# Scores of layer 0's paired panels on VectorE, the first panel's list one unit later, and lone panels normalized by VectorE, in a two-layer graph network with experts

## The chip, the cores and the metric

The kernel is one program on one core of a Trainium2 chip. The metric is the device time of one execution, in microseconds (us). The kernel before was timed three times: 1230.33, 1235.99 and 1239.86 us, median 1235.99 us. One further execution was taken by the hardware profiler; it took 1232.09 us and is the source of every duration below.

## The reference

There are N = 3327 nodes with D = 256 features, a dense matrix `adj` of 3327 x 3327 with few non-zeros, and two layers. Each layer is a graph step, followed by a step of 8 experts of which every node uses two.

```python
def _L0_gnn_ref(x, adj, W, b):
    return relu(matmul(adj, matmul(x, W)) + b)
def _L0_ffn_ref(x, Wg, bg, W1, b1, W2, b2):
    gate_scores = einsum('bsd,ed->bse', x, Wg) + bg      # 8 scores for each node
    topk_scores, topk_idx = top_k(gate_scores, 2)
    topk_probs = softmax(topk_scores, axis=-1)
    ...
    for e in range(8):
        h = relu(x @ W1[e].T + b1[e])                    # 256 -> 1024
        out = out + combine[..., e:e + 1] * (h @ W2[e].T + b2[e])
...
x = x + _L0_gnn_ref(_layernorm(x), adj, L0_gnn_W, L0_gnn_b)
x = x + _L0_ffn_ref(_layernorm(x), ...)
x = x + _L1_gnn_ref(_layernorm(x), adj, adj, ...)        # adjacency tanh(adj * adj), 700 largest of a row
x = x + _L1_ffn_ref(_layernorm(x), ...)                  # 8 experts, gelu, two of them for each node
```

The change touches layer 0's graph step and what is computed beside it for layer 0's experts: the normalization of the new `x`, the gate's scores, and the lists of nodes for each expert.

## The kernel before, in words

**Tiles, panels and units.** The nodes are padded to 3328, which is 26 tiles of 128. The graph step produces the output in 13 panels of 256 nodes (two tiles each). For one panel the kernel needs a strip of 3328 x 256 of `adj`, which it loads in two pieces of 13 x 256 columns per partition (1.66 MB each). Six such pieces fit in on-chip memory and form a ring; a piece's place is loaded again as soon as its last reader is done. Layer 0's panels are grouped into units: panels 0 and 1 alone, then the pairs (2,3), (4,5), (6,7), (8,9), (10,11), then panel 12 alone.

**The product of a lone panel** (`rest`, L495) is direct: 26 tiles times two halves of the features. **The product of a pair** (`pair`) uses a scheme of seven products in place of eight: sums and differences of the pieces of `adj` are made on VectorE (`add_pieces`, L480), those of the features once (`sum_features`), and the seven products (`product`, L470) are added up in four PSUM banks. Their results go to `g1` and `g2`, partly by copies on ScalarE (`copy`, L538), partly by corrections on VectorE (L587, L603, L604). A matmul in fp32 appears as two records of about 0.2157 us each.

**What follows a unit is done in the next one.** In the first product of a unit, after its matmuls 1, 4, 7 and 10, `weigh` multiplies the sums of the unit before by the layer's weights (L506, into two PSUM buffers) and `add_relu` (L403, L404, VectorE) adds the result to `x`. For a lone panel the same is done by `finish`, a few tiles after the unit's start. Then the following steps work on the tiles of the unit before:

- *Normalization* (`route0`, `normalized`): statistics on VectorE (L337 to L349), then `scaled` (L360), one operation per tile on ScalarE.
- *Scores.* For a pair, the first two tiles are scored on VectorE: one operation per tile and expert multiplies the normalized tile with the gate's row and sums it (L659; each is followed by a short read of the accumulator). The other two tiles are turned by TensorE (`turned_tiles`, L387, two transposes per tile), copied from PSUM by ScalarE (L388), multiplied with the gate's weights on TensorE (L669) and copied by VectorE (L678). For a lone panel both tiles are scored on VectorE.
- *Ranks and weights* (`weights`, L717 on): the two best scores of each node, and a softmax of the two, whose exponential is on ScalarE (L725).
- *List* (`list_tokens`), one unit later: GpSimd writes the weights, the node numbers and a second copy of the row beside the normalized rows (three copies, from L754 on), TensorE counts the places (L760, L761), VectorE makes indices of them (L762 to L768), and GpSimd issues four indirect DMAs for two tiles, which scatter the rows to the experts' lists in HBM (L779). After the list of panels 8 and 9 an early plan (`plan_early`) is made on VectorE and GpSimd, which assigns the first blocks of nodes to experts.

**Other work in the same stretch.** `count` (L1371, ScalarE) counts the positive entries of each raw piece before `add_pieces` overwrites it. `fill` writes zeros into the spare rows of a list: a memset, an iota and a copy on GpSimd, and 16 DMAs on SP's queue (L1334, L1336), which also loads the pieces of `adj`. `begin` calls it at panel 1 for layer 0's list and at panel 4 for layer 1's. Panel 12's unit is followed by the first step of layer 0's experts. Its 16 products of the first weight matrix (`ps_h`, L1171) go to two PSUM buffers and are evicted by ScalarE with the activation (L1178); the last panel's `finish` is called between this step's two halves.

**What sets the order.** The kernel is written in Python, and a scheduler orders the instructions of each engine according to their dependences and the order of the source. The source steers it by generators: `route0` is a generator with three `yield`s, and each `next(routing)` in `pair` puts the next part of it at that place among the products. Each engine then runs its instructions in order, so that an instruction that waits holds all behind it. Buffers are reused in rings: three for the normalized tiles `xn` (two tiles each), two of `ph` (for `ps_o`, `ps_h`), four of `py` (the sums), two of `pt` (transposes, scores, places).

Of the kernel before, what the change touches and what calls it, by code (L numbers as in the profile page):

```python
# [10 lines left out]
F32 = mybir.dt.float32  # L11
# [11 lines left out]
P = 128  # L23
# [3 lines left out]
DC = D // P  # L27
E = 8
# [99 lines left out]
def gnn_moe_two_layers(  # L128
# [353 lines left out]
    def aggregate_first(b_sb, w, w_sb, begin, count, route, listed, freed):  # L482
# [85 lines left out]
        def pair(p1, p2, ps_x, ps_q, ps_b, ps_z):  # L568
            a11, a12, a21, a22 = (piece(pan, k) for pan in (p1, p2) for k in range(NCHUNK))
            b11, b21, b22 = half(0, 0), half(1, 0), half(1, 1)  # L570
            t3, t2, t4, t1 = half_sums
            hooks, pans = finishing()
            product(ps_x, b11, a11, hooks=hooks)
            g1, g2 = sums_of(), sums_of()
            copy(g1[:, 0, :], ps_x)
            add_pieces(a11, a21)
            add_pieces(a21, a22)
            count_next()
            listed()
# [12 lines left out]
            free(p2, 0)  # L592
            product(ps_x, t2, a22, first=False)
            copy(g1[:, 1, :], ps_x)
            free(p2, 1)
            count_next()
            product(ps_z, b22, a12, first=False)
            free(p1, 1)
            count_next()
            product(ps_x, t3, a11, first=False, hooks={3: lambda: next(routing)})  # L600
            for _ in routing:
                pass
            nc.vector.tensor_tensor(g1[:, 1, :], g1[:, 1, :], ps_z, ALU.add)  # L603
            nc.vector.scalar_tensor_tensor(  # L604
                g2, g2, -1.0, ps_x.unsqueeze(1).to_broadcast([P, DC, PW]), ALU.mult, ALU.subtract
            )
            free(p1, 0)
            waiting.extend([(p1, g1), (p2, g2)])

# [134 lines left out]
    routed = []  # L744
# [607 lines left out]
    g1_wg_sb = const.tile([P, DC, D], F32, name="g1_wg_sb")  # L1352
    f1_r_sb = const.tile([P, DC, E], F32, name="f1_r_sb")
    f1_b1_sb = const.tile(list(f1_b1.shape), F32, name="f1_b1_sb")
    f0_wg_sb = const.tile([P, DC, E], F32, name="f0_wg_sb")
    g1_bp_sb = const.tile(list(g1_bp.shape), F32, name="g1_bp_sb")
    for t, w in [
        (gnn_b_sb, g0_b[0:1, :].partition_broadcast(P)),
        (g1_wg_sb, g1_wg.rearrange("(c p) n -> p c n", p=P)),
        (f1_r_sb, f1_rT.rearrange("(c p) n -> p c n", p=P)),  # L1360
        (f1_b1_sb, f1_b1),
        (g1_bp_sb, g1_bp),
        (f0_wg_sb, f0_wgT.rearrange("(c p) n -> p c n", p=P)),
    ]:
        follow(nc.gpsimd.dma_start(out=t, in_=w), last_normalized)

# [17 lines left out]
    def route0(pans):  # L1384
        if pans[0] == 0:
            load_gate(gates[0])
        t, n = tiles_of(pans)
        xns = normalized(t, n, on_scalar=True)
        yield
        by_product = 2 if n == 4 else 0  # L1390
        sc = scores(xns, n - by_product, n)
        yield
        if by_product:
            scores_by_product(by_features(xns[1], 2, "h2T"), 2, f0_wg_sb, sc[:, 2:4, :])
        yield
        routed.append((xns, *weights(sc, n, f0_bg_sb), t, n, xlist0, "0"))

    def listed0():
        if not routed:
            return  # L1400
        last = routed[-1][4] + routed[-1][5]
        list_waiting()
# [447 lines left out]
```

## Time and profile before

| what | value |
| --- | --- |
| three runs, us | 1230.33, 1235.99, 1239.86 |
| profiled execution, us | 1232.09 |
| its span, first to last instruction, us | 1230.4 |
| mean granted TensorE clock | 0.985 |
| TensorE busy, 0 to 104.1 us (panels 0 to 3) | 97.87 of 104.10 |
| TensorE busy, 104.1 to 289.1 us (pairs (4,5) to (10,11)) | 180.75 of 185.00, clock 0.98 |
| VectorE busy, 104.1 to 289.1 us | 135.70 |
| ScalarE busy, 104.1 to 289.1 us | 104.77 |
| TensorE busy, 289.1 to 360 us (panel 12, first expert steps) | 65.27 of 70.90, clock 0.98 |
| TensorE busy, 360 to 561 us (experts of layer 0) | 200.94 of 201.00, clock 1.00 |
| score operations L659 on VectorE, 104 to 360 us | 96, mean 443 ns; 96 reads of the accumulator, mean 81 ns |

How to read a profile of this kind: PE is TensorE, DVE is VectorE, ACT is ScalarE, POOL is GpSimd and SP the engine that issues most of the DMAs. A group of instructions is written with its line in the kernel, its operation, the tile that it writes and the tiles that it reads, the count (x), and busy time and mean. "Idle before" is the time for which the engine stood idle just before instructions of this group, and the arrow names the engine and line that ended the idle time. The granted clock is the share of TensorE's full rate that the throttle gave; where it is below 1.00, matmuls take longer, and TensorE still counts as busy. A table of stretches gives the length of each, and the busy time of each engine in it with the number of instructions.

### The profile page before, as it was taken

To read this page: it belongs to the slowest core of one execution; us is meant where nothing else is said; L and a number is where in the kernel's file an instruction comes from. 1 tells how busy PE (TensorE), PEld (TensorE's weight loads), DVE (VectorE), ACT (ScalarE), POOL (GpSimd) and SP (SyncE) were. 2 spreads that over 40 slices of the span, in tenths; PEclk is the share of its full clock that TensorE was granted. 3 is DMA by queue.
4 is the path that set the end of the run, shared out by engine and by line. 5 is a ranking of instruction groups with operands and counts; after the bars stand their busy time and mean duration, and the time that the engine had idled before them with its cause. 6 is when DMAs were issued, how large, how long until landed. Compare 5 with 4: busy or idle time off the path is not lost. (4 is left out here: it accounts for less than half of the span.)

```text
span 1230.4 us, 18162 instructions
## 1 busy us (share of the span) xinstructions
PE 1181.0 (96%) x5749; PEld 1010.8 (82%) x5749; DVE 719.5 (58%) x2609; ACT 531.0 (43%) x988; POOL 286.9 (23%) x368
## 2 busy tenths in 40 slices
PE   8999999999999999999999999999999999989973
PEld 7878888888878888888888888888888888868862
DVE  6797687596572111211111358389999998775454
ACT  5689556540222222222232235994554552033321
POOL 1212131242231111110111110004223233255531
PEclk9999999999999999999999999999999999999997
DMA  9899634534366556657575736235544551467796
GB/s 340 189 299 281 221 127 148 202 119 163 108 202 236 181 200 202 219 184 254 180 247 190 282 157 269 101 127 190 184 163 168 184 185 63 143 207 219 224 291 204
DMA packets 123209, 241.60 MB, mean 196 GB/s; under 512 B 24496, under 2 KB 93152, under 8 KB 116192
## 3 DMA queue, kind: packets, MB, share of 16 engines
q1 hardware_dynamic: 108656, 205.59, 51.1%
q0 software_dynamic: 11168, 31.61, 6.8%
q10 hardware_dynamic: 3280, 3.15, 0.7%
q8 instruction: 48, 0.79, 0.3%
q14 instruction: 57, 0.47, 0.1%
HBM read 203.99 MB, written 36.33 MB: 195 GB/s over the span
## 5 line engine op out<-in xcount | busy, mean ns | idle before, releaser
L440 PE MATMUL ps_g<-s,ring 128*128 128x256 f32 x1352 | 294.2, 380 | 0.0
L440 PEld LDWEIGHTS ps_g<-s,ring 128*128 128x128 f32 x1352 | 256.0, 190 | 34.4
L1178 ACT ACTIVATE pad<-ps_h,ring 128x256 f32<-128x256 f32 (+1 forms) x282 | 128.5, 457 | 331.0 <-PE ps_h L1171 309.0
L1171 PE MATMUL ps_h<-pad,ring 128*128 128x256 f32 (+1 forms) x1184 | 255.1, 368 | 8.8 <-ACT pad L1161 5.4
L1171 PEld LDWEIGHTS ps_h<-pad,ring 128*128 128x128 f32 x1184 | 203.3, 191 | 53.4 <-ACT pad L1178 14.6
L1209 PE MATMUL ps_y<-ring,pad 128*128 128x256 f32 x928 | 209.4, 381 | 0.0
L779 POOL DMA_INDIRECT ys<-pad,index x114 | 112.1, 983 | 387.4 <-DVE pad L1217 246.8
L1209 PEld LDWEIGHTS ps_y<-ring,pad 128*128 128x128 f32 x928 | 173.5, 191 | 22.2 <-ACT pad L1178 0.2
L659 DVE SCALAR_TENSOR_TENSOR rt_product<-xn,gate 128x256 f32<-128x256 f32 x320 | 160.6, 502 | 14.2 <-ACT xn L360 3.6
L779 POOL DMA_INDIRECT xlist<-xn,rt_idx x104 | 112.7, 1084 | 173.4 <-DVE ln_nw L347 52.0
L1371 ACT ACTIVATE sign<-ring,below 128x416 bf16<-128x416 f32 x208 | 133.4, 642 | 11.7 <-DMA ring<-in_adjT 5.8
L470 PE MATMUL ps_g<-ring,pad 128*128 128x256 f32 x520 | 121.0, 390 | 0.2 <-DMA ring<-in_adjT 0.2
L470 PEld LDWEIGHTS ps_g<-ring,pad 128*128 128x128 f32 x520 | 100.2, 195 | 14.4 <-DMA ring<-in_adjT 0.6
L1216 DVE TENSOR_TENSOR pad<-ps_y,ring 128x256 f32<-128x256 f32 x64 | 27.1, 423 | 137.3 <-PE ps_y L1209 133.5
L1540 ACT ACTIVATE ring<-ring 128x3328 f32<-128x3328 f32 x22 | 65.4, 2979 | 87.3 <-DVE ring L1539 56.3
L1161 DVE COPY pad<-ptb 128x512 f32<-128x512 f32 (+1 forms) x29 | 18.9, 653 | 143.5 <-PE ptb L1157 143.5
L470 PE MATMUL ps_g<-ring,s 128*128 128x256 f32 x390 | 90.6, 382 | 0.0
L470 PEld LDWEIGHTS ps_g<-ring,s 128*128 128x128 f32 x390 | 75.0, 192 | 10.5
L480 DVE TENSOR_TENSOR ring<-ring,ring 128x768 f32<-128x768 f32 (+1 forms) x80 | 79.8, 1014 | 0.4 <-ACT sign L1371 0.4
L495 PE MATMUL ps_g<-ring,s 128*128 128x256 f32 x312 | 70.4, 386 | 2.6 <-ACT s L360 2.6
L495 PEld LDWEIGHTS ps_g<-ring,s 128*128 128x128 f32 x312 | 59.9, 194 | 11.5 <-ACT s L360 3.2
L1541 ACT ACTIVATE ring<-ring 128x3328 f32<-128x3328 f32 x22 | 65.4, 2978 | 0.6
(224 smaller groups left out, 1119.5 us busy)
## 6 DMA issues: line engine op xcount, KB each, us to landing
ring<-in_adjT SPq DMA_DIRECT2D x50, 1664.0 KB
ring<-in_f_w1T SPq DMA_DIRECT2D x30, 1024.0 KB
ring<-in_f_w2T SPq DMA_DIRECT2D x30, 1024.0 KB
ring<-xlist SPq DMA_DIRECT2D x52, 258.0 KB
ring<-in_f_w SPq DMA_DIRECT2D x36, 256.0 KB
ring<-ys SPq DMA_DIRECT2D x12, 512.0 KB
ring<-in_f_b SPq DMA_DIRECT2D x34, 128.0 KB
xlist<-h2T SPq DMA_DIRECT2D x16, 257.0 KB
```

The lines of the kernel that those rows point to most:

```text
L440: nc.tensor.matmul(ps[it], lhsT=chunks[k][:, c, ts(it, P)], rhs=s[:, j, :], start=(j == 0), stop=(j == NT - 1),)
L470: nc.tensor.matmul(ps, lhsT=b[:, c, :], rhs=a[:, c, :], start=(first and c == 0), stop=(c == CJ - 1), skip_group_check=not first,)
L480: nc.vector.tensor_tensor(out[:, part, :], out[:, part, :], other[:, part, :], ALU.add)
L495: nc.tensor.matmul(sums[pan][c], lhsT=s[:, j, ts(c, P)], rhs=piece(pan, j // CJ)[:, j % CJ, :], start=(j == 0), stop=(j == NT - 1),)
L659: nc.vector.scalar_tensor_tensor(product, xn, 1.0, gate[:, e, :], ALU.mult, ALU.mult, accum_out=sc[:, g, e : e + 1],)
L779: d = nc.gpsimd.indirect_dma_start(out=a[:, :], out_offset=bass.IndirectOffsetOnAxis(ap=index, axis=0), in_=rows_, in_offset=None,)
L1171: nc.tensor.matmul(ps, lhsT=w1[:, c, ts(hc, P)], rhs=xT[:, c, :], start=(c == 0), stop=(c == DC - 1),)
L1178: nc.scalar.activation(hT[:, hc, :], ps, func, bias=bb1[:, hc : hc + 1])
L1209: last_product[:] = [nc.tensor.matmul(ps, lhsT=hT[:, hc, ts(g, P)], rhs=w2[:, hc, :], start=(hc == 0), stop=(hc == hc_n - 1),)]
L1371: nc.scalar.activation(sign, piece(pan, k)[:, :, ts(i, GROUP)], AF.Sign, bias=below, accum_out=positive[:, pan, i, k : k + 1],)
L1540: nc.scalar.activation(a, a, AF.Square)
L1541: nc.scalar.activation(a, a, AF.Tanh)
```

## The change

The change has six edits, all in layer 0's part.

1. All four tiles of a pair are scored on VectorE (L659): 32 operations per pair in place of 16. The transposes (L387), ScalarE's copy (L388), the product (L669) and VectorE's copy (L678) of a pair's last two tiles are left out, with the weights `f0_wg_sb` and their load.
2. In `pair`, the corrections of `g1` and `g2` are written ahead of the rest of `route0` (ranks and weights); the addition to `g1` comes straight after the sixth product, and the hook in the seventh product goes.
3. `route0` has two `yield`s in place of three, so that all scores are in one part.
4. The list of panel 0 is not made in the unit after its scores, but together with panel 1's, in the unit of pair (4,5).
5. Lone panels are normalized by VectorE (`layernorm`, L371 in the new file), pairs by ScalarE as before.
6. Layer 1's list is filled at panel 8 instead of panel 4.

```diff
@@ def pair
             product(ps_z, b22, a12, first=False)
             free(p1, 1)
             count_next()
-            product(ps_x, t3, a11, first=False, hooks={3: lambda: next(routing)})
+            nc.vector.tensor_tensor(g1[:, 1, :], g1[:, 1, :], ps_z, ALU.add)
+            product(ps_x, t3, a11, first=False)
+            nc.vector.scalar_tensor_tensor(
+                g2, g2, -1.0, ps_x.unsqueeze(1).to_broadcast([P, DC, PW]), ALU.mult, ALU.subtract
+            )
             for _ in routing:
                 pass
-            nc.vector.tensor_tensor(g1[:, 1, :], g1[:, 1, :], ps_z, ALU.add)
-            nc.vector.scalar_tensor_tensor(
-                g2, g2, -1.0, ps_x.unsqueeze(1).to_broadcast([P, DC, PW]), ALU.mult, ALU.subtract
-            )
             free(p1, 0)
             waiting.extend([(p1, g1), (p2, g2)])
@@ constants
-    f0_wg_sb = const.tile([P, DC, E], F32, name="f0_wg_sb")
...
-        (f0_wg_sb, f0_wgT.rearrange("(c p) n -> p c n", p=P)),
     ]:
         follow(nc.gpsimd.dma_start(out=t, in_=w), last_normalized)
@@ def route0, listed0, begin
         t, n = tiles_of(pans)
-        xns = normalized(t, n, on_scalar=True)
+        xns = normalized(t, n, on_scalar=n == 4)
         yield
-        by_product = 2 if n == 4 else 0
-        sc = scores(xns, n - by_product, n)
-        yield
-        if by_product:
-            scores_by_product(by_features(xns[1], 2, "h2T"), 2, f0_wg_sb, sc[:, 2:4, :])
+        sc = scores(xns, n)
         yield
         routed.append((xns, *weights(sc, n, f0_bg_sb), t, n, xlist0, "0"))
 
     def listed0():
-        if not routed:
+        if not routed or len(routed) == 1 and routed[0][4] == 0:
             return
         last = routed[-1][4] + routed[-1][5]
         list_waiting()
@@
     def begin(pan):
-        if pan in (1, 4):
+        if pan in (1, 8):
             fill(xlist0 if pan == 1 else xlist1)
```

In `pair`, `listed` is called after the first product and `route(pans)` after the second. The next parts of `route0` are asked for after the third product and (before the change) inside the seventh.

More of the change, by code (lines that the diff above doesn't have):

```diff
@@ L599, in pair @@
             count_next()
-            product(ps_x, t3, a11, first=False, hooks={3: lambda: next(routing)})
-            for _ in routing:
-                pass
             nc.vector.tensor_tensor(g1[:, 1, :], g1[:, 1, :], ps_z, ALU.add)
+            product(ps_x, t3, a11, first=False)
             nc.vector.scalar_tensor_tensor(
@@ L606, in pair @@
             )
+            for _ in routing:
+                pass
             free(p1, 0)
```

## The prediction, made before the result was known

> **What bounds the kernel now.** I read the shares of busy time first, then the stretches between the starts of consecutive pairs, then TensorE's list of waits, then the timelines of TensorE, VectorE and ScalarE around those waits.
>
> ```profile
> PE 1181.0 (96%) x5749; PEld 1010.8 (82%) x5749; DVE 719.5 (58%) x2609; ACT 531.0 (43%) x988; POOL 286.9 (23%) x368
> ...
> 104.10:149.60 45.50, 44.58 (x216) 38.95 (x216) 32.66 (x94) 34.47 (x93) 8.72 (x8) 1.00 0.72 209
> 149.60:197.30 47.70, 46.27 (x219) 40.17 (x218) 33.47 (x105) 27.32 (x74) 13.37 (x14) 0.96 0.48 166
> 197.30:245.50 48.20, 46.31 (x219) 40.30 (x218) 33.38 (x105) 27.31 (x74) 13.36 (x14) 0.96 0.48 164
> 245.50:289.10 43.60, 43.60 (x216) 38.28 (x215) 36.19 (x132) 15.67 (x42) 12.66 (x14) 1.00 0.46 154
> ```
>
> The columns are the stretch, its length, busy time of PE, PEld, DVE, ACT and POOL, granted clock, DMA share and GB/s. These are the pairs (4,5) to (10,11). TensorE is the bound, yet the same work takes 43.6 to 48.2 us; VectorE is busy for 33 us of each. The chain that ended last covers only the tail (from 1211 us) and says nothing of this stage, so I use the waits before 360 us and one of their places.
>
> ```profile
> PE pg L669 <- ACT h2T L388: 6.4, 4, 2.1
> PE ps_h L1171 <- ACT pad L1178: 3.0, 1, 3.0
> PE pr L760 <- DVE rt_both L697: 2.0, 1, 2.0
> ...
> 187.85 0.60 PE L387 MATMUL pt<-ident,xn 128*128 128x128 f32 x4
> 188.28 1.46 PE L470 MATMUL ps_g<-ring,pad 128*128 128x256 f32 x6
> 191.18 1.06 PE L669 MATMUL pg<-f_wg_sb,h2T 128*128 128x8 f32 x8 [1.44 <-ACT h2T L388]
> 192.09 4.52 PE L470 MATMUL ps_g<-ring,pad 128*128 128x256 f32 x12
> ...
> 192.10:194.00 1.90, 1.90 (x7) 0.55 0.23 98
> ```
>
> The reader is to see that the four score products hold TensorE for their copy (1.44 us here), and that the twelve matmuls behind take 4.52 us where 12 x 0.2157 = 2.6 us is the rate elsewhere (26 in 5.61 us): the clock column is at 0.55. The wait costs twice.
>
> ```profile
> 186.39 0.42 DVE L603 TENSOR_TENSOR xnT<-xnT,ps_g 128x256 f32<-128x256 f32 x1 [5.48 <-PE ps_g L470]
> 192.28 0.17 DVE L678 COPY rt_sc<-pg 128x16 f32<-128x16 f32 x1 [5.46 <-PE pg L669]
> ...
> 317.55 0.21 ACT L725 ACTIVATE rt_d<-rt_d 128x4 f32<-128x4 f32 x1 [8.89 <-DVE rt_d L724]
> 319.91 0.80 ACT L538 COPY xnT<-ps_g 128x256 f32<-128x256 f32 x2 [2.15 <-PE ps_g L495]
> ```
>
> VectorE sits idle for about 11 us of that pair, first for the product, then for the scores: this is the room for the added work. The last two lines matter below: the exponential of pair (10,11) now comes before the copies.
>
> [...] half-rate stretches of 3.41 us begin at 72.8, 192.3, 240.1 and 342.5 us, each soon after a gap of 1.8 to 3.4 us between matmul starts, while gaps of 1.3 us (at 143.8) and 2.4 us (at 306.3) brought none. One such stretch costs about 1.7 us, and whether a gap brings it is partly chance. [...] beside GpSimd's two row copies at 128.1 us two score operations took 0.70 us instead of 0.42.
>
> **The change, part by part.**
> *Products removed.* Measured from the trace, pair by pair (transposes, wait and product, half-rate excess): (4,5) 0.44 + 2.01 = 2.45 us; (6,7) 0.44 + 2.52 + 1.77 = 4.7; (8,9) 0.44 + 3.17 + 1.56 = 5.2; (10,11) 0.43 + 0.89 = 1.3. Sum 13.7 us, all on TensorE, and each pair comes down to about 43.0 us, the work alone. In panel 12's unit, from 304.06 to 309.63, 0.66 + 0.28 + 0.22 + 3.23 = 4.4 us.
>
> *Scores added.* 16 more operations per pair at a pitch of 0.467 us (with their accumulator reads; 16 ran from 173.40 to 180.92) are 7.5 us of VectorE. Does it fit? Per pair: from the last correction (L604) to the first score 24.35 us, less 1.43 of tail of the weights, which the new order puts before the correction: 22.9. Scores 32 x 0.47 = 15.0; g1's addition 0.34; ranks and weights 4.0; GpSimd's copies, which now fall beside scores, 2 x 0.28 = 0.6. Sum 42.9 us against TensorE's 43.0. VectorE starts pair (6,7) some 2 us late (two lists in the unit before it) and stays so; the correction is first needed about 5.2 us into the next pair (the third `weigh`). Hence no wait. In (10,11) the early plan adds 3.5 us: lag 4.5 to 6 us. There the next unit asks for the list only 5.2 us in, where VectorE idles 3.47 us today; I take 0.5 us (0 to 0.9).
>
> *The new wait.* In panel 12's unit the scores start 14.6 us in (303.72) and end 15.0 + 0.6 us later at 319.3; the exponent's input is ready 3.3 us after that, with the lag at about 323.2 us on the clock of the trace before. ScalarE meets this exponential after four evictions L1178 of the first expert, and four more evictions queue behind it; TensorE has two buffers for these. With its 4.4 us gained it needs the fifth eviction at about 320.9 and the seventh product stops near 321.4 until 323.9: a wait of 2.5 us (0 to 3.6). Half rate may follow: 0 or 1.7, I take 1.2. Together 0.5 + 2.5 + 1.2 = 4.2 against 4.4 gained: this unit gives 0.2.
>
> *First panel's list one unit later.* TensorE's gap at 69.7 is 2.25 us, and the 32 matmuls behind it took 8.87 instead of 6.9 + 0.1: 4.1 us. But the additions L480 on VectorE then come late: the third set is ready at 82.9 where its product could start at 82.2, the fourth at 88.9 for 88.5 after that. I give back 1.1 and count 3.0 us (2 to 4.1). The list's three GpSimd copies stay; its 4 scatters move past a pause of GpSimd to those of panel 1. Eight of them follow each other at 1.3 to 1.9 us; the second tile of the pair needs the first tile's buffer freed and is asked for 7.5 us after the scores begin, so this is free unless landing takes 8 us more.
>
> *Second fill moved.* Its memset, iota and copy stay at the head of GpSimd's queue. Its 16 DMAs leave SP's queue after the load at 103.46 and stand after the one at 196.65; they ran from 103.8 to 122 us, and the next load there is due 26.2 us later (222.88). Nothing queues behind them in that time: 0. If they were slower by half they would delay a load that is needed 20 us after its issue.
>
> *Lone panels on VectorE.* Two operations of 0.44 us less one shift of 0.16: +0.7 us on VectorE for each of three panels, less a pause of 0.7 us for ScalarE, which is freed of 2 x 0.59: 0. Corrections of g1 and g2 ahead of the weights: in the instruction order as built g2's still follows the weights; counted above. The gate's small load (L1365) is the last of its queue, behind which nothing waited: 0.
>
> **Sum**: 13.7 + 0.2 + 3.0 = 16.9 us. From 360 us on TensorE is busy 199.9 of 200 us and every load follows its steps, so the gain carries to the end. The profiled execution took 1232.1 us (span 1230.4 and 1.7 around it): 1215.2. The median of the three runs is 3.9 us higher; on it 1236.0 - 16.9 = 1219.
>
> **Rivals.** *Better (1209 to 1214, chance 0.15).* The pause of 3.0 us at 338, whose cause the trace doesn't show (its releaser is called remote), goes with its half rate, 4.9 us, or ScalarE's new wait doesn't come (3.7): 16.9 + 4.9 = 21.8, and both 25.5. Against it: the same scatters stand before the same step.
> *VectorE takes over in part (1224 to 1233, chance 0.22).* Lags of 5 us and more make the third `weigh` wait, with half rate behind it: 2 to 4 us in each of three pairs. For it: 42.9 against 43.0 leaves no reserve; against it: 3 us of slack at that place.
> *VectorE is the bound, and the kernel is slower (1255, chance 0.08).* If every score runs at the 0.75 us pitch seen beside GpSimd instead of 0.467, the unit is 42.9 + 32 x 0.28 = 51.9 us against a mean of 46.5 today: 5.4 x 4 = 21.6 slower, 3.0 saved, +19. It decides from 46.5 us on, 3.6 us above my count. Against it: only copies slowed scores, the eight scatters from 164 to 176 us did not.
>
> **Numbers.** Forecast 0.55 (1214 to 1223). A measurement tells about 1% (12.4 us). Faster by over 1% (below 1223.6): 0.52 + 0.15 = 0.67. Within: 0.03 + 0.22 and a bit of the slow tail, 0.26. Slower: 0.07. The range leaves out the slow case and the best end: 1209 to 1232.
>
> **What would show it.** Right: pairs of 43 us with the clock at 1.00, no L387 or L669 before 360 us, VectorE's idle time before L602 small, no wait for L697 near 70 us, a wait of L1171 for L1178 of some 2 us near 305. Wrong: TensorE waiting for L602 or L403 in the pairs, scores at a pitch above 0.6 us, or L659 waiting for L360 of a second tile.

## The result, and the profile after

The changed kernel took 1219.37, 1219.84, 1221.61 and 1222.40 us, median 1220.72 us; the kernel before, on the same chip, took 1235.38 us (median of four). The ratio is 0.9883, with a 95% interval of 0.9842 to 0.9924. The forecast was 1219 us, range 1209 to 1232.

The profiled execution tells less than the medians: it took 1222.40 us, the slowest of its four, against 1232.09 us, below three of the four of before. So the profiles differ by 9.7 us and the medians by 14.7.

The page's first lines for the changed kernel:

```profile
span 1220.7 us, 18191 instructions
...
PE 1176.8 (96%) x5689; PEld 1008.2 (83%) x5689; DVE 755.1 (62%) x2767; ACT 524.4 (43%) x977; POOL 288.2 (24%) x367
```

From its table of stretches, the pairs (4,5) to (10,11), the unit of panel 12 and the first expert block (columns as in the prediction: length, busy PE, PEld, DVE, ACT, POOL, clock, DMA share, GB/s):

```profile
100.70:143.70 43.00, 43.00 (x208) 37.83 (x207) 39.62 (x132) 33.99 (x94) 12.93 (x12) 1.00 0.53 191
143.70:186.70 43.00, 43.00 (x207) 37.86 (x206) 40.28 (x132) 26.00 (x71) 12.50 (x14) 1.00 0.52 184
186.70:229.70 43.00, 43.00 (x207) 37.84 (x206) 40.32 (x133) 26.74 (x73) 12.37 (x14) 1.00 0.75 230
229.70:271.90 42.20, 42.20 (x204) 37.14 (x204) 36.82 (x140) 18.66 (x51) 12.68 (x14) 1.00 0.44 148
271.90:302.30 30.40, 28.96 (x134) 24.54 (x133) 25.99 (x113) 2.54 (x6) 9.77 (x14) 0.94 0.48 165
302.30:329.40 27.10, 21.16 (x93) 17.17 (x91) 18.51 (x83) 4.74 (x13) 9.80 (x13) 0.87 0.16 51
```

The reader sees the pairs at 43.0 us with TensorE never idle and the clock at 1.00, VectorE busy for 40 us where it was 33, and then two stretches in which TensorE stands idle and its clock drops to means of 0.94 and 0.87. TensorE's list of waits of the changed kernel, from 50 to 360 us, names what stops it:

```profile
PE ps_h L1171 <- ACT pad L1178: 6.0, 2, 4.0
PE pr L760 <- DVE rt_both L697: 1.3, 1, 1.3
PE ps_g L470 <- DMA ring<-in_adjT: 0.5, 1, 0.5
```

No wait for L388's copy is left. From TensorE's timeline of the changed kernel, at the end of pair (10,11) and in the first expert block:

```profile
278.58 0.18 PE L760 MATMUL pr<-rt_both,before 128*128 128x8 bf16 x1 [1.32 <-DVE rt_both L697]
...
302.28 5.34 PE L1171 MATMUL ps_h<-pad,ring 128*128 128x256 f32 x24
311.63 3.78 PE L1171 MATMUL ps_h<-pad,ring 128*128 128x256 f32 x8 [4.01 <-ACT pad L1178]
```

And from ScalarE's, in the first expert block:

```profile
305.93 0.47 ACT L1178 ACTIVATE pad<-ps_h,ring 128x256 f32<-128x256 f32 x1 [0.39 <-PE ps_h L1171]
311.01 0.21 ACT L725 ACTIVATE rt_d<-rt_d 128x4 f32<-128x4 f32 x1 [4.61 <-DVE rt_d L724]
```

ScalarE stands for 4.61 us before the exponential of pair (10,11), with the fifth eviction queued behind it until 311.12 us; TensorE has two PSUM buffers for these and stops for 4.01 us. The eight matmul records behind that take 3.78 us, where 8 x 0.2157 = 1.7 us is the full rate: the granted clock is 0.50 from 310.60 to 317.43 us. Why the exponential was so late shows in VectorE's timeline of the changed kernel, among the scores of pair (10,11):

```profile
258.85 0.42 DVE L659 SCALAR_TENSOR_TENSOR rt_product<-xn,gate 128x256 f32<-128x256 f32 x1
259.20 0.08 DVE L659 DVE_READ_ACCUMULATOR rt_product<-xn,gate 128x1 f32 x1
263.33 0.17 DVE L1187 CAST index<-ring 128x2 int32<-128x2 f32 x1 [4.04 <-DMA ring<-xlist]
263.40 0.42 DVE L659 SCALAR_TENSOR_TENSOR rt_product<-xn,gate 128x256 f32<-128x256 f32 x1
```

The scheduler put the cast of the first expert block's row numbers (L1187) after the sixth score of pair (10,11), and the block's rows land 4.0 us after VectorE gets there. In the profile before, the cast stood at the same place and ran at 275.72 us with no wait. That profile is the exception, though: a second profile of the kernel before (c_before, below) has a wait there too. VectorE's timeline of c_before:

```profile
271.03 0.17 DVE L1187 CAST index<-ring 128x2 int32<-128x2 f32 x1 [3.35 <-DMA ring<-xlist]
```

So the change did not bring this wait. What it took away is the time that VectorE had in hand behind it: in both profiles of the kernel before, its last correction of the pair ends 4.3 us before the next unit's first `weigh`, in the changed kernel 1.6 us after it.

**Where the time went**, between marks on TensorE: first `weigh` of panel 0's sums, first `weigh` of pair (2,3)'s sums, start of the last matmul of the last pair, first matmul of layer 1's aggregation (L440), us. The first column holds the end of panel 1's unit and the unit of pair (2,3):

| profile | unit of pair (2,3) | pairs (4,5) to (10,11) | from there to L440 |
| --- | --- | --- | --- |
| before | 54.85 | 184.76 | 493.13 |
| changed | 51.45 | 171.03 | 497.64 |
| gain | 3.4 | 13.7 | -4.5 |

12.7 us are gained up to L440. From the last matmul of layer 1's aggregation to TensorE's last, the changed kernel's profile took 137.6 us (clock 0.94) where before took 132.8 (0.99); with 1.8 us back after it, 9.7 us are left at the end. That last stretch holds the same work in both.

### The profile page after: what moved, and what is told of

Its sections match the earlier page's. It is cut to its first block, busy times and chain, and to the rows that moved or that the text cites. A ratio compares the mean times of both kernels' runs of the same rounds, so it can differ in the third digit from the quotient of the medians.

```text
span 1220.7 us, 18191 instructions
## 1 busy us (share of the span) xinstructions
PE 1176.8 (96%) x5689; PEld 1008.2 (83%) x5689; DVE 755.1 (62%) x2767; ACT 524.4 (43%) x977; POOL 288.2 (24%) x367
## 5 line engine op out<-in xcount | busy, mean ns | idle before, releaser
L440 PE MATMUL ps_g<-s,ring 128*128 128x256 f32 x1352 | 294.2, 380 | 0.0
L440 PEld LDWEIGHTS ps_g<-s,ring 128*128 128x128 f32 x1352 | 256.3, 190 | 34.0
L1178 ACT ACTIVATE pad<-ps_h,ring 128x256 f32<-128x256 f32 (+1 forms) x282 | 128.3, 457 | 346.3 <-PE ps_h L1171 321.7
L1171 PE MATMUL ps_h<-pad,ring 128*128 128x256 f32 (+1 forms) x1184 | 259.0, 372 | 9.5 <-ACT pad L1178 6.0
L1171 PEld LDWEIGHTS ps_h<-pad,ring 128*128 128x128 f32 x1184 | 205.8, 193 | 55.0 <-ACT pad L1178 18.9
L659 DVE SCALAR_TENSOR_TENSOR rt_product<-xn,gate 128x256 f32<-128x256 f32 x400 | 195.1, 488 | 16.2 <-ACT xn L360 2.2
L470 PE MATMUL ps_g<-ring,pad 128*128 128x256 f32 x520 | 115.5, 380 | 0.7 <-DMA ring<-in_adjT 0.5
L470 PE MATMUL ps_g<-ring,s 128*128 128x256 f32 x390 | 89.6, 379 | 0.1
L480 DVE TENSOR_TENSOR ring<-ring,ring 128x768 f32<-128x768 f32 (+1 forms) x80 | 79.8, 1013 | 0.0
L495 PE MATMUL ps_g<-ring,s 128*128 128x256 f32 x312 | 68.5, 380 | 3.0 <-ACT s L360 3.0
```

Source lines behind the costliest of these rows:

```text
L440: nc.tensor.matmul(ps[it], lhsT=chunks[k][:, c, ts(it, P)], rhs=s[:, j, :], start=(j == 0), stop=(j == NT - 1),)
L470: nc.tensor.matmul(ps, lhsT=b[:, c, :], rhs=a[:, c, :], start=(first and c == 0), stop=(c == CJ - 1), skip_group_check=not first,)
L480: nc.vector.tensor_tensor(out[:, part, :], out[:, part, :], other[:, part, :], ALU.add)
L495: nc.tensor.matmul(sums[pan][c], lhsT=s[:, j, ts(c, P)], rhs=piece(pan, j // CJ)[:, j % CJ, :], start=(j == 0), stop=(j == NT - 1),)
L659: nc.vector.scalar_tensor_tensor(product, xn, 1.0, gate[:, e, :], ALU.mult, ALU.mult, accum_out=sc[:, g, e : e + 1],)
L1171: nc.tensor.matmul(ps, lhsT=w1[:, c, ts(hc, P)], rhs=xT[:, c, :], start=(c == 0), stop=(c == DC - 1),)
```

## The experiments

All ran where the kernel before takes 1211 to 1228 us in place of 1230 to 1240: e1 to e8 on one chip, c_before, c_after and c_best on another. Ratios are to the kernel before, timed beside each on the same chip. The sections of the table are compared across the two chips as well; one kernel, run on both (e6 and c_best), took 171.03 and 485.11 us on each. The three columns of the table of marks, for every profile that was taken there, with the ratio:

| profile | unit (2,3) | pairs | to L440 | ratio, 95% interval |
| --- | --- | --- | --- | --- |
| before (c_before) | 53.52 | 180.28 | 485.97 | |
| changed (c_after) | 52.44 | 171.03 | 494.64 | 0.9922 (0.9894 to 0.9950) |
| e1_scores_only | 54.45 | 170.93 | 493.20 | 0.9914 (0.9892 to 0.9937) |
| e2_list_only | 49.86 | 185.29 | 485.97 | 0.9965 (0.9947 to 0.9983) |
| e3_fill_norm_back | 56.23 | 171.03 | 492.78 | 0.9907 (0.9884 to 0.9930) |
| e4_cast_late | 50.12 | 171.03 | 489.57 | 0.9865 (0.9819 to 0.9910) |
| e5_exp_late | 54.68 | 171.03 | 489.84 | 0.9875 (0.9828 to 0.9922) |
| e6_cast_exp | 49.79 | 171.03 | 485.11 | 0.9849 (0.9807 to 0.9890) |
| e6 again (c_best) | 55.96 | 171.04 | 485.11 | 0.9859 (0.9830 to 0.9889) |
| e7_more_scores | 56.06 | 177.08 | 495.44 | 0.9992 (0.9978 to 1.0006) |
| e8_products_no_wait | 54.21 | 176.36 | 489.45 | 0.9937 (0.9919 to 0.9955) |

The first column differs by 6 us between two profiles of one kernel (49.79 and 55.96), at least in part since the first pieces and constants land at different times: c_best waits 4.4 us there for a piece. Only the other two columns are used to tell small edits apart. In e4, e5, e6, c_best and e8 added lines shift the line numbers: L1172, L1183 and L1184 are L1171 of the changed kernel, L1179 and L1191 its L1178, L737 its L725.

The third column can be cut further, at the first product of each of the first three expert blocks (us; "before" and "changed" are the first two profiles):

| profile | last pair to first block | first block | second block | from there to L440 |
| --- | --- | --- | --- | --- |
| before | 31.25 | 16.27 | 19.81 | 425.80 |
| changed | 30.57 | 23.30 | 17.12 | 426.65 |
| c_before | 29.02 | 16.27 | 14.87 | 425.81 |
| c_after | 30.54 | 22.56 | 14.87 | 426.66 |
| e4_cast_late | 26.84 | 21.20 | 14.87 | 426.66 |
| e5_exp_late | 31.26 | 17.04 | 14.87 | 426.67 |
| c_best | 26.84 | 16.74 | 14.87 | 426.67 |
| e8_products_no_wait | 26.84 | 21.08 | 14.87 | 426.66 |

The smallest figure of the first column, 26.84 us, is the work alone: the four profiles that show it (these three and e6) have no wait of TensorE there.

**c_before and c_after: both kernels, unchanged.**

> The kernel before, unchanged, profiled on the chip of the experiments. Theory (the pairs' units are the same on every chip, the losses behind the experts' first step and in the tail differ from execution to execution): pairs (4,5) to (10,11) at 45.4 to 48.2 us, start of layer 1's aggregation 777 to 782 us. Rival (this chip's shorter times lie in the pairs): pairs under 45 us.

> The changed kernel, unchanged, on the chip of the experiments. Theory: units of 43.0 us, the wait before L760 and the wait of L1171 for L1178 as in the first profile (1 to 2 us and 3 to 4 us, each with half rate behind it), but without the gap of 2.4 us at 327 us that four of the experiments don't show; start of layer 1's aggregation 763 to 768 us, ratio to the kernel before 0.987 to 0.990. Rival (the gap at 327 us belongs to the changed kernel): it is there again, 769.

Measured: pairs of 45.1, 46.0, 45.8 and 43.4 us before (the last one to its last matmul), 43.02 each and 41.97 after. The expectation for c_before was met in part: two of the first three pairs lie in its range and one just below, none under the rival's 45 us, but L440 began at 768.65 us and not at 777 to 782. Against the first profile 4.5 us of this lie in the pairs and 7.2 behind them, where that profile's gaps at 306 and 338 us are missing. Of the expectation for c_after, the pairs held and so did both waits (1.8 and 3.1 us); how much half rate stood behind each is not shown, but up to the first block it took 30.54 us and in it 22.56, which is 3.7 and 5.8 us more than in c_best, where neither wait occurs; L440 at 768.09 us is at the edge of the range, the ratio of 0.9922 is outside it, and the gap of 2.4 us at 327 us isn't there, so its rival falls. In c_before TensorE's clock stayed at 1.00 throughout the pairs, though its gaps of 1.74 and 1.55 us before the score products (1.36 and 1.17 us of them idle, by the lines below) were nearly as long as the 1.81 and 2.27 us of the first profile, each of which had half rate behind it (clock 0.50 from 192.30 and from 240.09 us, for 3.41 us each). From the table of stretches of c_before, the pairs (6,7) and (8,9):

```profile
147.50:193.50 46.00, 44.64 (x219) 39.02 (x219) 33.31 (x104) 27.33 (x74) 13.37 (x14) 1.00 0.49 172
193.50:239.30 45.80, 44.63 (x219) 39.02 (x218) 33.27 (x104) 27.33 (x74) 13.37 (x14) 1.00 0.50 173
```

And TensorE's list of waits of c_before:

```profile
PE pg L669 <- ACT h2T L388: 3.1, 3, 1.4
PE pr L760 <- DVE rt_both L697: 2.4, 1, 2.4
```

So the pairs' gain is 9.2 us here and 13.7 us in the first two profiles, and the 8.7 us that the stage behind gives back are nearly as much: 1.5 before the first block, 6.3 in it and 0.9 behind.

**e1: the scores alone**, in the kernel before.

```diff
-        by_product = 2 if n == 4 else 0
+        by_product = 0
```

> The kernel before with one edit: all four tiles of a pair are scored on VectorE; panel 0's list, the lone panels' normalization, the fill and the order of the corrections stay. Theory (the products' waits and half rate cost 13.7 us, and the list is a gain of its own of about 3): pairs (4,5) to (10,11) at 43.0 us each, the unit of pair (2,3) still about 54.9 us; start of layer 1's aggregation 3 to 3.5 us later than in the changed kernel (772 to 773 us). Rival (the order of the corrections is what makes the scores fit): the correction of g2 comes late, TensorE waits for it in each pair, pairs of 44 us or more.

Measured: pairs 170.93 us, as in the changed kernel, and the unit of pair (2,3) 54.45, so the theory holds there. L440 was expected 3 to 3.5 us later than in the changed kernel; it began at 767.87 us against 768.09 in c_after. That part missed: the first column is 2.0 us longer than in c_after, but what follows the pairs is 1.4 us shorter. The ratio, 0.9914, is no worse than that of the whole change, 0.9922 (0.9894 to 0.9950): on these chips the other five edits add nothing to the first that can be told from noise. The order of the corrections makes no difference to the pairs: in both kernels VectorE's timelines show the correction of g2 behind the ranks, at the weights (L604 at 147.40 us in e1, L602 at 146.60 in c_after, each straight after L729). The rival falls.

**e2: the list alone**, in the kernel before.

```diff
     def listed0():
-        if not routed:
+        if not routed or len(routed) == 1 and routed[0][4] == 0:
```

> The kernel before with one edit: panel 0's list is made together with panel 1's, in the unit of pair (4,5). Theory: the gap of 2.4 us before L760 at 69.6 us and the half rate behind it go, the unit of pair (2,3) comes from 54.9 down to 51.5 us, and no later unit changes by itself: 3 us (2 to 4.1) at the start of layer 1's aggregation (779). Rival: the late additions L480 or the eight scatters of two lists give it back: under 1 us.

Measured: the unit of pair (2,3) took 49.86 us, with no wait for L697 and no half rate (from 65 to 100 us TensorE busy 35.00 us at a clock of 1.00); c_before took 53.52, with a wait of 2.4 us at that place and none of the half rate (32.56 us busy, clock 1.00). The ratio is 0.35% (0.17 to 0.53) below one, 4.3 us (2.1 to 6.4). The theory holds, and the late additions give nothing back here (e7 and e8, which have this edit too and in which the bias of `add_relu` landed latest, wait 2.1 us for L480). The gap before L760 near 70 us is in all three profiles with the old place of the list (before, c_before, e1: 2.0 to 2.4 us) and in none of the ten with the new one; half rate followed it in the first (clock 0.50 from 72.83 to 76.24 us) and not in c_before. (L440 at 770.59 us is later than in c_before: the pairs took 5.0 us more, of which 1.6 are the waits for L388, 4.7 us in place of 3.1. The other 3.4 us would be two stretches of half rate (3.41 us at a clock of 0.50, so 1.7 us each), an estimate.)

**e3: fill and lone panels' normalization taken back**, in the changed kernel.

```diff
-        if pan in (1, 8):
+        if pan in (1, 4):
...
-        xns = normalized(t, n, on_scalar=n == 4)
+        xns = normalized(t, n, on_scalar=True)
```

> The changed kernel with two edits taken back: layer 1's list filled at panel 4 again, lone panels normalized by ScalarE again. Theory (both cost and gain nothing): within 1 us of the changed kernel up to the start of layer 1's aggregation (769.3), units of 43.0 us. Rival (the fill's 16 DMAs in the stretch of pair (8,9) delay the loads and scatters that the early blocks wait for): VectorE's wait of 4.0 us for the first block's rows, the wait before L760 at 277 us and the half rate behind it shrink, 3 us faster. Rival the other way: with the fill at panel 4 a load of a piece comes late: a wait of L470 for a DMA.

Measured: pairs 171.03 us and no wait for a load of theirs, so the second rival falls. The waits in the stage behind stay (L1171 3.1 us, L760 1.8), so the first rival falls too. L440 began at 768.83 us against 768.09 in c_after, within the 1 us of the theory, but not because nothing moved. From the last pair to L440 e3 is 1.9 us shorter than c_after. Of this, 0.9 us lies behind the second expert block and comes back everywhere: 425.8 us in all five profiles with the fill at panel 4 (before, c_before, e1, e2, e3), 426.7 in all eight with it at panel 8. So the two edits are not quite free together; that it is the fill and not the normalization is not shown. And before the pairs there is a wait that no part of my sum had. TensorE's list of waits of e3:

```profile
PE ps_o L506 <- ACT xnT L538: 4.6, 1, 4.6
```

And ScalarE's timeline of e3 at that place:

```profile
60.82 1.09 ACT L360 ACTIVATE xn<-x,ln_shift,ln_guess 128x256 f32<-128x256 f32 x2 [10.64 <-DVE ln_shift L354]
61.82 0.62 ACT L538 COPY xnT<-ps_g 128x256 f32<-128x256 f32 x2
```

Panel 1's copy L538 is queued on ScalarE behind panel 0's normalization, which waits for VectorE, which waits for the bias of `add_relu` to be loaded. With ScalarE normalizing, L538 came 6.2 us after the first L403 in each of five profiles: L403 at 51.7 to 51.9 us left at most 1.1 us between two matmul starts there, at 53.2 us 2.0 and at 55.7 us 5.0. In the eight with VectorE normalizing and L403 at 52.4 to 58.4 us L538 started at 56.5 to 57.5 us whatever the bias; only in e7, with the latest bias, TensorE waited 1.2 us there, for L403 itself. So this edit, which I put at nothing, takes away a wait that grows with a late bias, 4.6 us in e3. Whether that shortens the whole is not shown: in c_after, e5 and c_best TensorE waited 2.5 to 4.4 us for a piece of `adj` some 7 us later, where e3 waited for none, and the first column is no shorter with VectorE normalizing (49.8 to 56.1 us) than with ScalarE (49.9 to 56.2).

**e4: the cast later**, in the changed kernel.

```diff
-            nc.vector.scalar_tensor_tensor(
+            corrected[:] = [nc.vector.scalar_tensor_tensor(
                 g2, g2, -1.0, ps_x.unsqueeze(1).to_broadcast([P, DC, PW]), ALU.mult, ALU.subtract
-            )
+            )]
...
-            with behind(last_y):
+            with behind(last_y or corrected):
                 if t < EARLY:
                     nc.vector.tensor_copy(index, xb[:, :, ID])
```

> The changed kernel, with the cast of the first expert block's row numbers (L1187) ordered behind the correction of g2 of pair (10,11) instead of among its scores, where VectorE waits 4.0 us for the block's rows to land. Theory (this wait, not the early plan's 3.5 us alone, makes the ranks late): the wait of 1.3 us before L760 at 277 us and the half rate behind it go, 3 us earlier at the first product of the experts (302.3 to 299.3); the exponential comes 3 to 4 us earlier as well, so the wait of L1171 for L1178 stays near 4 us: 2 to 4 us at the start of layer 1's aggregation (769.3 to 766). Rival (the early plan alone made it late): no change of the wait before L760.

Measured: VectorE's wait for the rows is gone, TensorE's wait before L760 and the half rate behind it too (26.84 us up to the first block, as in c_best with a clock of 1.00), and the wait for the evictions stays. TensorE's list of waits of e4:

```profile
PE ps_h L1172 <- ACT pad L1179: 3.1, 1, 3.1
```

From the last pair to L440 489.57 us against c_after's 494.64: 5.1 us, more than the 2 to 4 I expected. Of this, 3.7 us lie before the first block (26.84 us against 30.54) and 1.4 in it (21.20 us against 22.56), with the same wait of 3.1 us. ScalarE's timeline of e4 shows half rate behind it: two evictions start 1.70 us apart (307.24 and 308.94 us) in place of 0.87. That it lasted longer in c_after is an estimate from the 1.4 us. The rival (the early plan alone) falls.

**e5: the exponential later**, in the changed kernel: ranks and weights of pair (10,11) are asked for in the next `finish`, and what they issue on ScalarE is ordered behind the first block's evictions.

```diff
-            for _ in route([pan for pan, _ in todo]):
+            routing = route([pan for pan, _ in todo])
+            if len(todo) == 2:
+                next(routing)
+                next(routing)
+                held.append(routing)
+                return
+            for _ in routing:
                 pass
...
             waiting.clear()
+            with behind(evicted):
+                while held:
+                    for _ in held.pop():
+                        pass
             listed()
```

> The changed kernel, with ranks and weights of pair (10,11) asked for later, so that its exponential (L725) follows the eight evictions L1178 of the first expert block instead of standing after four of them. Theory (in-order ScalarE waiting for VectorE is what stops TensorE there): the wait of 4.0 us of L1171 for L1178 at 307 us and the two stretches of half rate behind it go, first to last product of the first block in 6.9 us instead of 13; 5 to 7.5 us at the start of layer 1's aggregation (762 to 764). Rival (the exponential only shows a lateness that the next step meets anyway: the list of pair (10,11), its scatters or TensorE's count L760): the wait moves to L760, less than 2 us gained.

Measured: the wait for the evictions is gone, the eight evictions follow each other every 0.87 us, and the exponential stands behind them at no cost. ScalarE's timeline of e5:

```profile
313.15 0.47 ACT L1191 ACTIVATE pad<-ps_h,ring 128x256 f32<-128x256 f32 x1 [0.39 <-PE ps_h L1183]
313.99 0.21 ACT L737 ACTIVATE rt_d<-rt_d 128x4 f32<-128x4 f32 x1 [0.37 <-DVE rt_d L736]
```

489.84 us to L440, 4.8 us less than c_after and just short of the 5 to 7.5 expected. The theory holds in kind: the first block takes 17.04 us in place of 22.56. Nothing moved to the list of pair (10,11); the earlier wait before L760 (2.0 us here) is as it was.

**e6 and c_best: both moves**, one kernel, run twice.

> The changed kernel with both moves, the cast of the first block behind the correction of pair (10,11), and the exponential behind the first block's evictions. Theory: the two losses of the stage are separate and add up, 8 to 11 us at the start of layer 1's aggregation (758.5 to 761.5), median of the whole 1210 to 1213 us. Rival (one cause behind both): no more than the better of the two alone.

> The changed kernel with both moves (the cast of the first block and the exponential of pair (10,11)), again, beside the changed kernel on the same chip. Theory: 6 to 9 us below the changed kernel at the start of layer 1's aggregation and in the whole, no TensorE wait over 0.5 us between 107 and 345 us. Rival (the lower time of the first look was the execution's luck): less than 3 us between the two.

Measured: 485.11 us to L440 in both, 9.5 us less than c_after (5.1 and 4.8 alone make 9.9), and 0.9 us less than c_before. In the table of stretches of c_best, panel 12's unit and the first block have TensorE busy throughout:

```profile
234.00:276.20 42.20, 42.20 (x205) 37.10 (x204) 40.56 (x153) 18.65 (x51) 12.90 (x14) 1.00 0.41 141
276.20:302.90 26.70, 26.70 (x134) 23.43 (x134) 23.73 (x105) 2.54 (x6) 9.97 (x14) 1.00 0.56 197
302.90:321.30 18.40, 18.27 (x93) 15.47 (x92) 16.93 (x77) 4.96 (x12) 7.37 (x9) 1.00 0.19 64
```

The two losses are separate and add up. (For e6 I had put the median of the whole at 1210 to 1213 us, from the first profiles' times; it was 1199.68.) The medians are 1199.56 us for this kernel and 1208.49 for the changed one, timed together: 8.9 us. It beats both kernels, with ratios of 0.985 and 0.986 to the kernel before.

**e7: eight more scores per pair**, in the changed kernel.

```diff
         sc = scores(xns, n)
+        if n == 4:
+            scores(xns, 1)
         yield
```

> The changed kernel with eight more score operations for each pair (the first tile is scored twice, the second result unused): 8 x 0.467 = 3.7 us more on VectorE per pair. Theory of the prediction (42.9 us of VectorE work in each 43.0, no reserve but 3 us of slack once): pair (4,5) stays near 43, each later pair takes 46 to 47 us, TensorE waits for L602 or L403, half rate joins: 10 to 16 us later at the start of layer 1's aggregation. Rival (VectorE has idle time left, 40.3 us busy of 43.0): 43 to 44.5 us per pair, 1 to 5 us in all.

Measured: pairs (4,5) and (6,7) 43.02 us each, (8,9) 45.2 us, (10,11) 3.9 us longer than in the changed kernel; the whole as slow as the kernel before (0.9992), where the changed kernel stands at 0.9922: some 8 us given back. That is between the theory (10 to 16) and its rival (1 to 5), and TensorE waits for VectorE as the theory said, from pair (8,9) on; TensorE's list of waits of e7, and its timeline at the start of pair (8,9):

```profile
PE pr L760 <- DVE rt_both L697: 5.8, 2, 4.6
PE ps_o L506 <- DVE gnn_t L403: 4.9, 3, 1.9
...
197.40 1.13 PE L506 MATMUL ps_o<-proj_sb,xnT 128*128 128x256 f32 x4 [1.81 <-DVE gnn_t L403]
```

Of the three waits for L403, two are at the third `weigh` of pairs (8,9) and (10,11), 1.8 and 1.9 us; the first is the late bias at 57 us. How late VectorE is shows in the end of the correction L602, counted from the next pair's first `weigh`. In the changed kernel it is 1.9, 2.2 and 2.6 us from pair to pair, in e7 3.1, 5.4 and 5.5 us. At 3.1 TensorE did not wait, at 5.4 it waited 1.8 us: by that difference a lag of some 3.5 us is free (an estimate). From one L602 to the next VectorE takes 43.4 us in the changed kernel against TensorE's 43.02, and 45.4 in e7: the eight added scores lengthen its round by 2.0 us and not by the 3.7 of the theory, which is why the loss stayed below it. Where the other 1.7 us were saved is not shown.

**e8: the removed matmuls back, without their waits**, in the changed kernel.

```diff
-            product(ps_x, t3, a11, first=False)
+            product(ps_x, t3, a11, first=False, hooks={3: idle_products})
...
+        def idle_products():
+            ...
+                    nc.tensor.transpose(pt[:, c, ts(g, P)], x[:, 0, ts(c, P)], ident)
+            ...
+                    nc.tensor.matmul(
+                        pg[:, g, :], lhsT=ident, rhs=ident[:, 0:E], start=(c == 0),
+                        stop=(c == DC - 1),
+                    )
```

> The changed kernel with the removed matmuls put back without their waits: in the seventh product of each pair four transposes and four score products that read constants and an old tile, their results unused. Theory (of the 13.7 us of the products the waiting and the half rate are 11, the work 0.6 to 0.7 per pair): pairs (4,5) to (10,11) at 43.6 to 43.8 us, 3 to 3.5 us later at the start of layer 1's aggregation, pair (2,3) included; no half rate in the pairs. Rival (switching to small matmuls breaks TensorE's rhythm or its clock by itself): 44.5 us or more per pair.

Measured: 44.35 us per pair, 1.33 more than without, at a clock of 1.00. Both sides missed the size: the theory is 0.6 us too low, and the rival's mark of 44.5 isn't reached. TensorE's timeline of e8:

```profile
142.38 0.60 PE L517 MATMUL pt<-ident,x 128*128 128x128 f32 x4
142.82 0.96 PE L520 MATMUL pg<-ident 128*128 128x8 f32 x8
143.63 4.13 PE L470 MATMUL ps_g<-ring,pad 128*128 128x256 f32 x18
```

And PEld's, the loads of the weights:

```profile
142.71 0.97 PEld L520 LDWEIGHTS pg<-ident 128*128 128x128 f32 x8
```

The transposes take 0.44 us from start to start, as before. The score product has only eight columns, but each of its eight records has its own load of 128x128 weights. The eight loads take 0.97 us and the eight records follow each other every 0.10 us: 0.8 us, not 0.2. So of the 13.7 us that the products cost in the first profile, 4 x 1.33 = 5.3 us were work and 8.4 us were the waits for ScalarE's copy and the half rate behind them.

The 5.3 us did not reach L440, where 3 to 3.5 were expected: from the pairs' start to L440 e8 takes 665.8 us and c_after 665.7. With TensorE at 44.35 us per pair VectorE's lag stays at 0.2 to 0.6 us. Its wait for the first block's rows is still there, 3.25 us, but TensorE's wait before L760 is gone and the stretch up to the first block takes 26.84 us, as with the cast moved. So it takes both, the lag and the cast's wait, to stop TensorE there.

## Why the prediction was right, point by point, and where it was wrong

- **Products removed, 13.7 us: right, 13.7 measured** between the marks. What I didn't say is that a part of it was that execution's own: 3.3 of the 13.7 (1.77 and 1.56) was half rate (clock 0.96 in both pairs), which c_before lacks (1.00), and the waits there were shorter too, so that the change gains 9.2 us in its pairs. e1 shows that the scores' edit brings all of the pairs' gain by itself, and e8 that 5.3 us of it are work.
- **Scores fit on VectorE: right, with less reserve than I thought.** I counted 42.9 us per pair and measured 43.4; I put the lag at 2 us and measured 1.9 to 2.6. I took 3 us of slack beyond that, since the correction is first needed 5.2 us into the next pair. That is 4.3 us after the first `weigh`, from which the lags are counted, and by e7 the third `weigh` waits not for the correction alone but for the L403 that VectorE runs after it. So the slack was 0.9 to 1.6 us. The rival in which VectorE takes over in part did not come, but eight more scores per pair bring it. The slow rival, with all scores at 0.75 us, fell: 2 of a pair's 32 scores were slow. (The mean unit before, which decides it, is 46.25 us by the four stretches shown, not 46.5.)
- **The new wait: right in mechanism, too small in size.** ScalarE, the exponential and the fifth eviction were named. I put 2.5 us (0 to 3.6) and 1.2 for half rate. The first profile shows 4.0 us with 6.83 us at a clock of 0.50 behind it, twice 3.41, 7.0 us more than before in the first block; of the six later profiles with all scores on VectorE and the exponential in its old place, five wait 2.9 to 3.1 us, inside the range (the first block takes 21.1 to 22.6 us in three of them, e8, e4 and c_after, against 16.74 in c_best; what the wait leaves of this, 1.2 to 2.7 us, would be half rate, an estimate), and the sixth (e7, in which TensorE comes late itself) does not wait.
- **The step that failed is the wait before L760, and behind it the count of VectorE's work in pair (10,11)**: "In (10,11) the early plan adds 3.5 us: lag 4.5 to 6 us", for which I took 0.5 us (0 to 0.9). L760 waited 1.3 us in the first profile and 1.8 in c_after, and the stretch up to the first block took 30.6 and 30.5 us where the work is 26.84: 3.7 us. The count had the plan's operations, but not that the cast L1187 waits for a DMA in the middle of the scores. From the profile before this couldn't be read: its cast did not wait. It waits in every other profile in which it stands there, the kernel before included (c_before 3.35 us, e2 3.25), and in the changed kernel 4.0 and 4.6. Two things set the profile before apart from the changed one. In the changed one the scatters that the rows' load waits for start 1.3 us later after the pair's start, and the last of them takes 2.8 us in place of 1.4 (why isn't shown). e4 shows that without the cast's wait L760 does not wait, early plan or not; e8 shows that without VectorE's lag the cast's wait does no harm. e4's evictions still waited 3.1 us, so the exponential's place is a loss of its own, which e5 shows.
- **This unit gives 0.2: wrong, the stage lost 4.5 us** in the first pair of profiles and 8.7 in the second. The 4.4 us to be gained were counted rightly for that execution (31.25 - 4.4 is the 26.84 of e4 and c_best), but 2.2 of them were a wait for L388 that c_before lacks. In the first pair of profiles 2.7 us of the loss were hidden in the second block: the gap at 338 us and its half rate, 4.9 us in the kernel before, became a gap of 2.4 us at 327 us without half rate (clock 1.00 from 323 to 341 us). In none of the later profiles is such a gap there, in either kernel; its cause stays open.
- **First panel's list, 3.0 us: right in mechanism, its size not settled.** The first pair of profiles gives 3.4 us in a column that moves by 6 us between two profiles of one kernel. e2 alone gives 4.3 us (2.1 to 6.4), but on top of the scores no gain shows (e1).
- **Second fill and lone panels 0: nearly right.** Taken back together they leave the pairs as they are and gain 0.9 us behind the second expert block (e3). For the lone panels I weighed one pause of ScalarE against VectorE's longer work, and not what is queued on ScalarE behind the waiting normalization: up to 4.6 us of wait, of which it isn't shown that it counts in the whole.
- **The sum.** On the profile I had 16.9 us, 1215.2; it gave 9.7, 1222.4. The stage behind the pairs accounts for 4.7 of the difference, the last stretch of layer 1, where TensorE's clock was lower in that profile (0.94 against 0.99), for most of the rest. The later profiles c_before and c_after don't show that last difference (126.5 and 127.4 us, clock 0.99 in both), so I don't put it down to the change. That the median came within 2 us of 1219 is in part luck: the profiles to which the sum belongs differ by 9.7 us and the medians by 14.7, and where the later runs were made the change is worth 0.8% (0.5 to 1.1), 8.1 us between the medians.

## What to carry to other kernels

When work moves to an engine that has room, ask not only whether its busy time fits, but what it will now reach early or late: a cast that could wait 3.4 us for its data while VectorE had idle time behind it (c_before) held up TensorE once scores filled that time. The engines ran their instructions in order here (4.04 us of wait on VectorE and 4.61 on ScalarE held all that stood behind), so an operation with a late input belongs behind the operations that others wait for; two such moves here brought 8.9 us, as much as the change itself on that chip (1216.6 to 1208.5 us). Of a wait in one profile, separate the wait from the half rate behind it, which need not come back. And take more than one profile of the kernel before: the cast's wait, which decided this stage, was missing in the one that the prediction was made from.

## What the runs showed of the hardware that I had not expected

- Half rate, a granted clock of 0.50, came in stretches of 3.41 us or twice that up to 360 us. It came behind gaps between matmul starts of 1.70 us (276.88 us in the changed kernel; 0.50 from 279.88 to 283.29 us), 1.81 and 2.27 us (before; 0.50 from 192.30 and 240.09 us), and not behind 1.74 and 1.55 us (c_before), behind the wait of 2.4 us before L760 in c_before (1.00 from 65 to 100 us) or behind 2.36 us (changed, 327 us).
- That is less a matter of chance than the prediction says, by the clock records and the matmul starts of the first two profiles. The starts of the half-rate stretches of one profile are whole multiples of 3.413 us apart (35, 14 and 30 of them between 72.8, 192.3, 240.1 and 342.5 us before, 9 between 279.9 and 310.6 us in the changed kernel). If both profiles are cut at this pitch and TensorE's idle time (from matmul start to matmul start, less the usual distance) is summed in each piece, there are 683 pieces at full rate from 20 us on. Of those with less than 1.5 us of idle time, over 660, none was followed by half rate; all seven with 2.1 us or more were; between the two, those with 1.60, 2.05 and 2.08 us were and the rest, 1.89 and 1.93 us among them, were not. So in these two profiles it counts how a gap falls on the pieces: the 2.36 us at 327 us of the changed kernel, 2.14 us of them idle, are split into 1.89 and 0.25 us and brought none; the 1.70 us fell into one piece, with other short waits 2.08 us in all, and brought one. The gap of 4.39 us at 307 us filled 3.1 us of one piece and reached into the next, and half rate lasted for two (310.60 to 317.43 us).
- Eight fp32 products of eight columns take 0.8 us from start to start, near the 0.97 us of their eight loads of weights (e8, 142.82 and 142.71 us).
- Two runs of one program, on two chips, differ by 6 us in the unit of pair (2,3) (e6 49.79 and c_best 55.96 us), and the bias was first used, as soon as it had landed, at 51.66 us in e2, 51.91 before, 54.04 in the changed kernel and 55.66 in e3.
